# A two-layer kernel: input products issued three groups ahead in the scan layer, and the last convolution of the spectral layer on two row halves

## The chip, the cores and the metric

The kernel runs on one core of a Trainium2 chip. The metric is the device time of one execution in microseconds (us). The engines are named as in the profile: PE is TensorE (PEld its weight loads), DVE is VectorE, ACT is ScalarE, POOL is GpSimd and SP is SyncE, which here only issues DMAs.

## The reference

The input x is 4 images of 192 channels of 128 x 128, in fp32. Two residual layers follow each other, each on a group-normalised x (32 groups of 6 channels):

```python
x = x + L0(_gn(x), ...)     # spectral convolution
x = x + L1(_gn(x), ...)     # selective scan over the 16384 tokens of an image
```

The first layer (layer 1 in this text) reduces 192 channels to 48 by a 1x1 convolution. 16 of them get a 1x1 convolution, 16 a two-dimensional fractional Fourier transform, and 16 a real FFT; of both transforms magnitude and phase are convolved and transformed back. A last 1x1 convolution maps the 48 channels back to 192. The second layer (layer 2) normalises each token, projects it to 2 x 384 channels (xs and z), convolves xs along the tokens (4 taps), applies SiLU (u), computes dt, B and C from u, and runs for each of 384 channels and 16 states

```python
hnew = hcar * exp(dt_t * A) + (dt_t * u_t) * B_t
y_t  = sum over the 16 states of hnew * C_t
```

The result y + u * D is gated by SiLU(z) and projected back to 192 channels.

## The kernel before

**Layer 1** (`layer0` in the code) works image by image, a piece being 8 rows (1024 pixels of all 192 channels, 768 KB). `analysis(b)` reads the 16 pieces of an image twice: once for the statistics (`bn`), once for the first convolution (L278), whose result goes to HBM as d1. `branches(b)` computes the transforms, with several trips through HBM, and ends by writing the image dimg (L453). `synthesis(b)` reads each piece a third time, loads the 48 convolved channels and a row of ones into a tile cat (L464 to L466), multiplies it with the weights w2x (L471), adds the result to the piece (L475), takes the statistics for layer 2, and stores the piece (L477). The loop at L489 advances `branches(b)` step by step, and with it `analysis(b+1)` and `synthesis(b-1)`; here a scheduler orders the instructions of each engine. `synthesis` of the last image runs alone. Pieces come from a pool of 6 buffers.

**Layer 2** (`layer1` in the code) cuts the 4 x 16384 tokens into 128 chunks of 512. A chunk has 24 groups k, which are 3 channel tiles j by 8 pairs of states sg, so k = 8 j + sg. Here the order of every engine's queue is the order of the code (`manual_schedule`). For each state, ACT computes da = exp(dt A) (L802), DVE the scan over 512 tokens (`scans`, L872). The other input of the scan, (dt u) B, has three sources: POOL computes it for the pair as db (`inputs`, L830) in the groups 1, 4, 7, 9, 15, 17 and 23; PE transposes it back from a version that ACT scaled (`scale_pair` L846, `turned_back` L858) in the groups with sg = 3 and 6; and DVE multiplies it (`product`, L822) in the others. After a group's two scans POOL multiplies their result h with C, giving hc (L885). PE adds the hc of the 16 states into py by transposing matmuls (`sums`, L898), three groups later (LAG). `add_skip` (L912) adds u D, `evacuate` (L907) copies py to yt, `turn` (L922) turns it back, `gate` (L927) multiplies it with SiLU(z), and `finish` (L936) projects it. The tile h has 3 buffers, hc 5, db 2, and bc (the rows of B and C of a pair, spread over all partitions, L776) 8.

Into these groups the code weaves the parts of `front`, which prepares a later chunk: statistics of the tokens, projection, convolution, dt, B and C. `front` is a generator; a plain `yield` ends its part of a group, and what follows `yield MID` is issued after the group's first scan, what follows `yield LATE` at the group's end. The scaling of a chunk by its standard deviations (L660) is such a part.

What a group issues, in order, and where the distances to other groups are set:

```python
if pos >= LAG and sg != LAG:
    sums(*order[pos - LAG])
...
if pos + 2 < len(order):
    inputs(*order[pos + 2])
...
scans(pos, n, k, between)
...
if pos >= LAG and sg == LAG:
    sums(*order[pos - LAG])
    add_skip(n, j)
```

Of the kernel before, what the change touches and what calls it, by code (L numbers as in the profile page):

```python
# [19 lines left out]
C = 192  # L20
CH = 96
# [100 lines left out]
def layer0(tc, x, xmid, st2, w):  # L122

    nc = tc.nc
    B = x.shape[0]
    with ExitStack() as ctx:
        def pool(name, bufs, **kw):
            return ctx.enter_context(tc.tile_pool(name=name, bufs=bufs, **kw))

        cp = pool("l0c", 1)  # L130
        dram = pool("l0d", 2, space=DRAM)
        xp = pool("l0x", 6)
        sp = pool("l0s", 2)
        imp = pool("l0i", 2)
        zp = pool("l0z", 2)
# [13 lines left out]
        ri_cat, ri_out = const("ri_cat"), const("ri_out")  # L149


        w2x = cp.tile([3 * NC + 1, C], F32, name="w2x")
        nc.sync.dma_start(out=w2x[NC : 3 * NC, :], in_=w["w2T"][NC:, :])
# [6 lines left out]
        nc.sync.dma_start(out=w2x[0:NC, :], in_=folded[0:NC, :])  # L160
        nc.sync.dma_start(out=w2x[3 * NC :, :], in_=folded[NC:, :])
        half_pi = cp.tile([128, 1], F32, name="half_pi")
        nc.vector.memset(half_pi, math.pi / 2)

# [4 lines left out]
        dmag = []  # L169
        zrow = cp.tile([1, S], F32, name="zrow")  # L170
        nc.vector.memset(zrow, 0.0)
        orow = cp.tile([1, PIECE], F32, name="orow")
        nc.vector.memset(orow, 1.0)
# [73 lines left out]
        def analysis(b, got):  # L247


            st = sp.tile([CH, 2, NPIECE * (PIECE // 512), 6], F32, name="st")  # L250
            for p in range(NPIECE):
                bn(st, p, load(b, p))
                yield
            gst = sp.tile([CH, 2, 2], F32, name="gst")
            bn_done(st, gst)

            w1r = sp.tile([CH, 2, 128], F32, name="w1r")
            for t in range(2):  # L260
                nc.vector.tensor_scalar(w1r[:, t, :], w1T[:, t, :], gst[:, t, 1:2], None, ALU.mult)
            ps = psA.tile([128, 512], F32, name="ps")
            for t in range(2):
                nc.tensor.matmul(
                    ps[:, 0:1], w1r[:, t, :], gst[:, t, 0:1], start=t == 0, stop=t == 1
                )
            b1 = sp.tile([128, 1], F32, name="b1")
            nc.vector.tensor_scalar(b1, ps[:, 0:1], -1.0, None, ALU.mult)
            d1 = got["d1"] = dram.tile([3 * NC, S * S], F32, name="d1")
            for p in range(NPIECE):  # L270
                xt = load(b, p)
                if p % 2 == 0:
                    x1 = sp.tile([128, 2, 512], F32, name="x1")
                ps = psA.tile([128, 512], F32, name="ps")
                for t in range(2):
                    for q in range(2):
                        half = slice(64 * q, 64 * (q + 1))
                        nc.tensor.matmul(  # L278
                            ps[half], w1r[:, t, half], xt[:, t, q * 512 : (q + 1) * 512],
                            start=t == 0, stop=t == 1,  # L280
                        )
# [174 lines left out]
        def synthesis(b, got):  # L456

            d1, dimg = got["d1"], got["dimg"].rearrange("c h w -> c (h w)")
            st = sp.tile([CH, 2, NPIECE * (PIECE // 512), 6], F32, name="st2")
            for p in range(NPIECE):  # L460
                xt = load(b, p)
                cat = qp.tile([3 * NC + 1, PIECE], F32, name="cat", bufs=2)
                at = slice(p * PIECE, (p + 1) * PIECE)
                nc.sync.dma_start(out=cat[0:NC, :], in_=d1[0:NC, at])  # L464
                nc.sync.dma_start(out=cat[NC : 3 * NC, :], in_=dimg[:, at])
                nc.sync.dma_start(out=cat[3 * NC :, :], in_=orow)  # L466
                for q in range(PIECE // 512):
                    at = slice(q * 512, (q + 1) * 512)
                    pr = psB.tile([128, 2, 512], F32, name="pr")
                    for t in range(2):  # L470
                        nc.tensor.matmul(  # L471
                            pr[0:CH, t, :], w2x[:, t * CH : (t + 1) * CH], cat[:, at],
                            start=True, stop=True,
                        )
                    nc.vector.tensor_add(xt[:, :, at], xt[:, :, at], pr[0:CH])  # L475
# [12 lines left out]
        behind = iter(())  # L488
        for b in range(B):  # L489
            ahead = analysis(b + 1, got[b + 1]) if b + 1 < B else iter(())  # L490
            for i, _ in enumerate(branches(b, got[b])):
                next(ahead, None)
                next(ahead if i % 2 else behind, None)
            for rest in (behind, ahead):
                for _ in rest:
                    pass
            behind = synthesis(b, got[b])
        for _ in behind:
            pass

# [3 lines left out]
def layer1(tc, xmid, out, st2, w, n_tok=S * S):  # L504
# [2 lines left out]
    B = len(xmid)  # L507
    NCHUNK = n_tok // T
    G = 2
    LAG, FRONT, BCL = 3, 14, 5  # L510
    AHEAD = 4

    BY_POOL = ((1, 4, 7), (1, 7), (1, 7))
# [5 lines left out]
    with ExitStack() as ctx:  # L519
# [84 lines left out]
        def front(i):  # L604
# [51 lines left out]
                    rb[0:CH, q * 128 : (q + 1) * 128], sel[:, q, :], rows, start=True, stop=True  # L656
                )
            yield
            yield MID
            nc.vector.tensor_tensor(s, s, _bc(rb[0:CH], 1, 2), ALU.mult)  # L660
            yield

# [161 lines left out]
        def inputs(n, k):  # L824

            if by_pool(k):
                g = got[n]
                j, sg = divmod(k, NG)
                db = g["db", k] = scp.tile([128, G, T], F32, name="db", bufs=2)
                nc.gpsimd.tensor_tensor(db, _bc(g["dtu"][j], 1, G), g["bc", sg][:, 0], ALU.mult)  # L830
# [121 lines left out]
        def start_front(n):  # L952
            if n < total:
                fronts.append(front(n))
# [10 lines left out]
        def go_on(parts, part):  # L965

            for f in parts[part]:
                got_on = next(f, None)
                if got_on is not None:
                    parts[got_on].append(f)  # L970

        with tc.manual_schedule():
            for i in range(min(2, total)):
                load_x(i)
            for _ in front(0):
                pass
            for sg in range(NG):
                load_bc(0, sg)
            dtu_copy(0, 0)
            inputs(*order[1])  # L980
            for at in range(AHEAD):
                early(at)
            for s in range(2):
# [1 line left out]
            decay_there(2)  # L985


            start_front(1)
            for _ in range(NGR - FRONT):
                parts = {MID: [], LATE: []}  # L990
                step(fronts, parts)
                go_on(parts, MID)
                go_on(parts, LATE)
            tails = []
            for pos, (n, k) in enumerate(order):
                j, sg = divmod(k, NG)
# [9 lines left out]
                    gate(*before)  # L1006
                if sg + 1 in BY_PE:
                    turned_back(G * (pos + 1))
                if pos >= LAG and sg != LAG:
                    sums(*order[pos - LAG])  # L1010
                if k in TURNED:
                    turned(n, TURNED[k])
# [177 lines left out]
```

## Time and profile before

| | us |
|---|---|
| median of 3 executions | 11457.8 (11452.5 to 11463.0) |
| the profiled execution | 11449.6, span 11447.4 |
| layer 1, up to the last store of a piece | 1436 |
| of it, the last image's synthesis alone | 114 |
| from there to the first scan of layer 2 | 79 |
| one chunk of layer 2, of 128 | 77.5 |

The profile shows one execution. Busy time is time in which an engine has an instruction in work. The idle time before an instruction is put down to what released it, as told by semaphores; where an instruction waits for several, the last one is named.

### The profile page before, as it was taken

How to read it: one execution, taken by the hardware profiler on the slowest of the kernel's cores; microseconds unless marked ns; L12 is line 12 of the kernel's file. 1: busy time of each engine (PE TensorE's matmuls, PEld its weight loads, DVE VectorE, ACT ScalarE, POOL GpSimd, SP SyncE). 2: the span in 40 equal slices, each digit the busy share in tenths (PEclk: the TensorE clock that was granted, in tenths of full speed). 3: DMA queues.
4: the chain of work that ended last, by engine and by line, in shares of the span. 5: the costliest groups of instructions: out<-in, count | busy, mean ns of one | idle time of the engine just before them, and what ended most of it. 6: DMA issues, size and time to landing. Idle time of an engine off the chain costs nothing.

```text
span 11447.4 us, 163662 instructions
## 1 busy us (share of the span) xinstructions
PE 10543.1 (92%) x54154; PEld 7050.4 (62%) x54154; DVE 10489.8 (92%) x11072; ACT 9324.7 (81%) x17508; POOL 9806.5 (86%) x4470
## 2 busy tenths in 40 slices
PE   4777889999999999999999999999999999999998
PEld 2444456666666666666666666666666666666666
DVE  5665679999999999999999999999999999999999
ACT  2322179988988998998998998898899999889887
POOL 0000069999999999999999999999999999999999
PEclk8888789999999999999999999999999999999998
DMA  8787734334334434434433433443443443344343
GB/s 209 206 223 203 196 106 128 112 119 128 118 113 128 127 106 130 128 107 124 128 112 119 128 120 111 128 127 105 129 128 109 123 128 114 117 128 121 111 128 99
DMA packets 1339431, 1494.73 MB, mean 131 GB/s; under 512 B 903473, under 2 KB 954358, under 8 KB 1338070
## 3 DMA queue, kind: packets, MB, share of 16 engines
q1 hardware_dynamic: 1318102, 1421.34, 42.7%
q0 software_dynamic: 13312, 50.34, 1.3%
q10 hardware_dynamic: 7168, 12.59, 0.3%
q8 instruction: 429, 7.03, 0.2%
q14 instruction: 420, 3.44, 0.1%
HBM read 1325.19 MB, written 155.32 MB: 129 GB/s over the span
## 4 chain that ended last, share of the span: by engine, by line
ACT 29%; DVE 29%; PE 26%; issue 10%; POOL 3%; DMA 2%; DVEq 0%; ACTq 0%; POOLq 0%; SPq 0%
DVE h L872 21%; ACT da L802 9%; ACT dbT L846 6%; DVE op L822 6%; PE py L898 5%; PE ps L666 4%; PE ps L936 4%; PE ps L685 4%; ACT L802 3%; PE op L858 2%; POOL db L830 2%; ACT op L802 2%; PE pr L471 2%; ACT L693 1%; PE ps L655 1%
## 5 line engine op out<-in xcount | busy, mean ns | idle before, releaser
L885 POOL TENSOR_TENSOR hc<-h,bc 128x1024 f32<-128x1024 f32 x3072 | 7196.8, 2373 | 230.7 <-PE ps L922 145.6
L872 DVE TENSOR_TENSOR_SCAN h<-da,carry,op 128x512 f32<-128x512 f32 x4216 | 5202.2, 1262 | 18.7 <-ACT da L802 7.1
L898 PEld LDWEIGHTS py<-ident,hc 128*128 128x128 f32 x24576 | 3001.5, 148 | 849.3 <-issue 685.1
L898 PE MATMUL py<-ident,hc 128*128 128x128 f32 x24576 | 3404.1, 285 | 29.9 <-ACT yt L907 17.5
L802 ACT ACTIVATE da<-dt,c_A_log 128x512 f32<-128x512 f32 x4352 | 2994.6, 724 | 184.3 <-DVE h L872 163.6
L872 DVE TENSOR_TENSOR_SCAN h<-op,carry,db 128x512 f32<-128x512 f32 x1736 | 2202.3, 1269 | 119.2 <-POOL db L830 115.2
L830 POOL TENSOR_TENSOR db<-dtu,bc 128x1024 f32<-128x1024 f32 x896 | 2136.3, 2384 | 5.6 <-DMA bc<-dbc 5.6
L822 DVE TENSOR_TENSOR op<-dp,bc 128x512 f32<-128x512 f32 x2816 | 1889.9, 671 | 32.2 <-ACT dp L785 32.2
L802 ACT ACTIVATE op<-dt,c_A_log 128x512 f32<-128x512 f32 x1792 | 1223.2, 683 | 679.7 <-DVE h L872 674.4
L846 ACT ACTIVATE dbT<-ps,bT 128x128 f32<-128x128 f32 x6144 | 1660.3, 381 | 0.0
L666 PE MATMUL ps<-s,c_wiT 96*128 96x512 f32 x3072 | 1520.9, 619 | 2.6 <-DVE s L660 2.6
L685 PE MATMUL ps<-xs,dcw 128*128 128x512 f32 x3072 | 1424.3, 592 | 1.5 <-ACT u L693 1.3
L858 PE MATMUL op<-ident,dbT 128*128 128x128 f32 x6144 | 1076.2, 295 | 109.9 <-DVE h L872 75.5
L858 PEld LDWEIGHTS op<-ident,dbT 128*128 128x128 f32 x6144 | 779.8, 151 | 405.5 <-ACT dbT L846 208.7
L666 PEld LDWEIGHTS ps<-s,c_wiT 96*128 96x128 f32 x3072 | 558.1, 199 | 467.2 <-issue 462.9
L802 ACT ACT_TABLE_LOAD x636 | 816.0, 1283 | 11.2
L685 PEld LDWEIGHTS ps<-xs,dcw 128*128 128x128 f32 x3072 | 532.9, 190 | 434.1 <-issue 432.1
L936 PE MATMUL ps<-yg,c_woT 128*96 128x512 f32 x1536 | 710.5, 598 | 71.1 <-DVE xm L942 70.9
L477 POOL DMA_DIRECT2D xmid<-xt x64 | 42.8, 668 | 788.1 <-DVE xt L475 781.3
L745 PE MATMUL ps<-xd,c_dtT 12*128 12x512 f32 x768 | 514.1, 761 | 164.5 <-DVE s L622 99.7
L936 PEld LDWEIGHTS ps<-yg,c_woT 128*96 128x96 f32 x1536 | 239.8, 163 | 437.8 <-issue 320.7
L754 POOL TENSOR_TENSOR dtu<-dt,u 128x512 f32<-128x512 f32 x384 | 479.4, 1282 | 29.6 <-ACT dt L750 29.6
(172 smaller groups left out, 10372.6 us busy)
## 6 DMA issues: line engine op xcount, KB each, us to landing
bc<-dbc SPq DMA_DIRECT2D x1024, 1024.0 KB, 5.9
xt<-in_x SPq DMA_DIRECT2D x192, 768.0 KB, 9.0
xmid<-xt POOLq DMA_DIRECT2D x64, 768.0 KB, 7.0
xm<-xmid SPq DMA_DIRECT2D x128, 384.0 KB, 3.5
carry<-h SPq DMA_DIRECT2D x3072, 1.0 KB, 1.9
out<-xm SPq DMA_DIRECT2D x128, 384.0 KB, 3.3
d<-x ACTq DMA_DIRECT2D x64, 192.0 KB, 7.1
df<-u SPq DMA_DIRECT2D x16, 512.0 KB, 5.2
```

Source lines behind the costliest of these rows:

```text
L666: nc.tensor.matmul(pp, wiT[:, t, m * 128 : (m + 1) * 128], s[:, t, :], start=t == 0, stop=t == 1)
L685: nc.tensor.matmul(pc, dcw[:, j, k, :], xs[:, j, k : k + T], start=k == 0, stop=k == 3)
L745: nc.tensor.matmul(d[j], dtT[rows, :], xd[rows, :], start=True, stop=True)
L802: nc.scalar.activation(da, got[n]["dt"][j], AF.Exp, scale=A[:, j, st : st + 1])
L822: nc.vector.tensor_tensor(dbs[s], g["dp"], g["bc", k % NG][:, 0, q, :], ALU.mult)
L830: nc.gpsimd.tensor_tensor(db, _bc(g["dtu"][j], 1, G), g["bc", sg][:, 0], ALU.mult)
L846: nc.scalar.activation(t[:, blk, :], g["tu", j][:, blk, :], AF.Identity, scale=g["bT"][:, blk, st : st + 1],)
L858: nc.tensor.transpose(db[:, blk * 128 : (blk + 1) * 128], t[:, blk, :], ident)
L872: nc.vector.tensor_tensor_scan(h[:, q, :], das.pop(s), dbs.pop(s) if db is None else db[:, q, :], 0.0 if ch == 0 else g["before"][:, j, st ...
L885: nc.gpsimd.tensor_tensor(hc, h, g["bc", sg][:, 1], ALU.mult)
L898: nc.tensor.matmul(py[:, blk, :], hc[:, q, blk * 128 : (blk + 1) * 128], ident, start=first, stop=sg == NG - 1 and q == G - 1 and blk == T ...
L936: nc.tensor.matmul(po[0:CH], woT[:, j, t * CH : (t + 1) * CH], g["yg", j], start=j == 0, stop=j == NJ - 1,)
```

## The change

In layer 2:

- `inputs`, the product db on POOL, is issued three groups ahead of its scan instead of two.
- `sums` comes at the head of every group; before, it came at the end in the groups with sg = 3. `add_skip` stays at the end of those.
- The scaling L660 moves from after the first scan of its group to the group's end.
- The rows bc are loaded one group earlier (BCL 6 for 5).
- Before the first chunk's groups, the first ten steps of the second chunk's `front` are issued among the last part of the first chunk's, not after it.

In layer 1:

- cat becomes a tile of 128 partitions by 512: the first 512 pixels of a piece lie in the partitions from 0, the other 512 in those from 64, each with a row of ones that is set once. w2x is there twice in the same way. The matmuls of the last convolution read one half each and write a bank each, and the addition takes one half of the channels and all 1024 pixels.
- In `analysis`, the last 4 pieces of the first reading stay in their buffers for the second. The pool has 7 buffers.
- In the last image's stage `synthesis` of the image before advances at every step, and after step 18 four pieces of the last image are loaded.

```diff
-        xp = pool("l0x", 6)
+        xp = pool("l0x", 7)
...
+        cats = [cp.tile([128, 512], F32, name=f"cat{i}") for i in range(2)]
+        for cat in cats:
+            nc.vector.memset(cat, 1.0)
...
             for p in range(NPIECE):
-                bn(st, p, load(b, p))
+                xt = load(b, p)
+                if p >= NPIECE - KEEP:
+                    kept[p] = xt
+                bn(st, p, xt)
                 yield
...
-            for p in range(NPIECE):
-                xt = load(b, p)
+            for p in (*range(NPIECE - KEEP, NPIECE), *range(NPIECE - KEEP)):
+                xt = kept.pop(p, None) or load(b, p)
...
-                xt = load(b, p)
-                cat = qp.tile([3 * NC + 1, PIECE], F32, name="cat", bufs=2)
-                at = slice(p * PIECE, (p + 1) * PIECE)
-                nc.sync.dma_start(out=cat[0:NC, :], in_=d1[0:NC, at])
-                nc.sync.dma_start(out=cat[NC : 3 * NC, :], in_=dimg[:, at])
-                nc.sync.dma_start(out=cat[3 * NC :, :], in_=orow)
-                for q in range(PIECE // 512):
-                    at = slice(q * 512, (q + 1) * 512)
+                xt = early[p] if p < len(early) else load(b, p)
+                cat = cats[p % 2]
+                for q in range(2):
+                    at = slice(p * PIECE + q * 512, p * PIECE + (q + 1) * 512)
+                    nc.sync.dma_start(out=cat[64 * q : 64 * q + NC, :], in_=d1[0:NC, at])
+                    nc.sync.dma_start(out=cat[64 * q + NC : 64 * q + 3 * NC, :], in_=dimg[:, at])
+                for t in range(2):
                     pr = psB.tile([128, 2, 512], F32, name="pr")
-                    for t in range(2):
+                    for q in range(2):
+                        rows = slice(64 * q, 64 * q + 3 * NC + 1)
                         nc.tensor.matmul(
-                            pr[0:CH, t, :], w2x[:, t * CH : (t + 1) * CH], cat[:, at],
+                            pr[0:CH, q, :], w2x[rows, t * CH : (t + 1) * CH], cat[rows, :],
                             start=True, stop=True,
                         )
...
-                next(ahead if i % 2 else behind, None)
+                next(ahead if i % 2 and b < B - 1 else behind, None)
+                if b == B - 1 and i == LOADS:
+                    early = [load(b, p) for p in range(KEEP)]
...
-    LAG, FRONT, BCL = 3, 14, 5
+    LAG, FRONT, BCL = 3, 14, 6
...
-            yield MID
+            yield LATE
             nc.vector.tensor_tensor(s, s, _bc(rb[0:CH], 1, 2), ALU.mult)
...
-            for _ in front(0):
-                pass
-            for sg in range(NG):
-                load_bc(0, sg)
+            first = [front(0)]
+            for i in range(2 * NGR - FRONT):
+                if i == NGR - 6:
+                    start_front(1)
+                once(first)
+                if NGR - 6 <= i < 2 * NGR - FRONT - 6:
+                    once(fronts)
+                if i == NGR + 1:
+                    for sg in range(NG):
+                        load_bc(0, sg)
...
-                if pos >= LAG and sg != LAG:
+                if pos >= LAG:
                     sums(*order[pos - LAG])
...
-                if pos + 2 < len(order):
-                    inputs(*order[pos + 2])
+                if pos + 3 < len(order):
+                    inputs(*order[pos + 3])
...
-                if pos >= LAG and sg == LAG:
-                    sums(*order[pos - LAG])
+                if sg == LAG:
                     add_skip(n, j)
```

More of the change, by code (lines that the diff above doesn't have):

```diff
@@ L125, in layer0 @@
     B = x.shape[0]
+    KEEP = 4
+    LOADS = 18
     with ExitStack() as ctx:
@@ L149, in layer0 @@
         ri_cat, ri_out = const("ri_cat"), const("ri_out")
-        w2x = cp.tile([3 * NC + 1, C], F32, name="w2x")
-        nc.sync.dma_start(out=w2x[NC : 3 * NC, :], in_=w["w2T"][NC:, :])
+        w2x = cp.tile([128, C], F32, name="w2x")
+        for q in range(2):
+            nc.sync.dma_start(out=w2x[64 * q + NC : 64 * q + 3 * NC, :], in_=w["w2T"][NC:, :])
         w20, c0 = cp.tile([NC, C], F32, name="w20"), const("c0")
@@ L159, in layer0 @@
         nc.vector.tensor_copy(folded, ps[0 : NC + 1, 0:C])
-        nc.sync.dma_start(out=w2x[0:NC, :], in_=folded[0:NC, :])
-        nc.sync.dma_start(out=w2x[3 * NC :, :], in_=folded[NC:, :])
+        for q in range(2):
+            nc.sync.dma_start(out=w2x[64 * q : 64 * q + NC, :], in_=folded[0:NC, :])
+            nc.sync.dma_start(
+                out=w2x[64 * q + 3 * NC : 64 * q + 3 * NC + 1, :], in_=folded[NC:, :]
+            )
         half_pi = cp.tile([128, 1], F32, name="half_pi")
@@ L171, in layer0 @@
         nc.vector.memset(zrow, 0.0)
-        orow = cp.tile([1, PIECE], F32, name="orow")
-        nc.vector.memset(orow, 1.0)
+        cats = [cp.tile([128, 512], F32, name=f"cat{i}") for i in range(2)]
+        for cat in cats:
+            nc.vector.memset(cat, 1.0)
         for i in range(min(2, B)):
@@ L250, in analysis @@
             st = sp.tile([CH, 2, NPIECE * (PIECE // 512), 6], F32, name="st")
+            kept = {}
             for p in range(NPIECE):
-                bn(st, p, load(b, p))
+                xt = load(b, p)
+                if p >= NPIECE - KEEP:
+                    kept[p] = xt
+                bn(st, p, xt)
                 yield
@@ L454, in branches, with synthesis @@
             got.update(dimg=dimg)
-        def synthesis(b, got):
+        def synthesis(b, got, early):
             d1, dimg = got["d1"], got["dimg"].rearrange("c h w -> c (h w)")
@@ L460, in synthesis @@
             for p in range(NPIECE):
-                xt = load(b, p)
-                cat = qp.tile([3 * NC + 1, PIECE], F32, name="cat", bufs=2)
-                at = slice(p * PIECE, (p + 1) * PIECE)
-                nc.sync.dma_start(out=cat[0:NC, :], in_=d1[0:NC, at])
-                nc.sync.dma_start(out=cat[NC : 3 * NC, :], in_=dimg[:, at])
-                nc.sync.dma_start(out=cat[3 * NC :, :], in_=orow)
-                for q in range(PIECE // 512):
-                    at = slice(q * 512, (q + 1) * 512)
+                xt = early[p] if p < len(early) else load(b, p)
+                cat = cats[p % 2]
+                for q in range(2):
+                    at = slice(p * PIECE + q * 512, p * PIECE + (q + 1) * 512)
+                    nc.sync.dma_start(out=cat[64 * q : 64 * q + NC, :], in_=d1[0:NC, at])
+                    nc.sync.dma_start(out=cat[64 * q + NC : 64 * q + 3 * NC, :], in_=dimg[:, at])
+                for t in range(2):
                     pr = psB.tile([128, 2, 512], F32, name="pr")
-                    for t in range(2):
+                    for q in range(2):
+                        rows = slice(64 * q, 64 * q + 3 * NC + 1)
                         nc.tensor.matmul(
-                            pr[0:CH, t, :], w2x[:, t * CH : (t + 1) * CH], cat[:, at],
+                            pr[0:CH, q, :], w2x[rows, t * CH : (t + 1) * CH], cat[rows, :],
                             start=True, stop=True,
                         )
-                    nc.vector.tensor_add(xt[:, :, at], xt[:, :, at], pr[0:CH])
+                    nc.vector.tensor_add(
+                        xt[:, t, :], xt[:, t, :], pr[0:CH].rearrange("p q f -> p (q f)")
+                    )
                 bn(st, p, xt)
@@ L490, in layer0 @@
             ahead = analysis(b + 1, got[b + 1]) if b + 1 < B else iter(())
+            early = []
             for i, _ in enumerate(branches(b, got[b])):
                 next(ahead, None)
-                next(ahead if i % 2 else behind, None)
+                next(ahead if i % 2 and b < B - 1 else behind, None)
+                if b == B - 1 and i == LOADS:
+                    early = [load(b, p) for p in range(KEEP)]
             for rest in (behind, ahead):
@@ L496, in layer0 @@
                     pass
-            behind = synthesis(b, got[b])
+            behind = synthesis(b, got[b], early)
         for _ in behind:
@@ L970, in go_on, with once @@
                     parts[got_on].append(f)
+        def once(works):
+            parts = {MID: [], LATE: []}
+            step(works, parts)
+            go_on(parts, MID)
+            go_on(parts, LATE)
         with tc.manual_schedule():
@@ L974, in layer1 @@
                 load_x(i)
-            for _ in front(0):
-                pass
-            for sg in range(NG):
-                load_bc(0, sg)
+            first = [front(0)]
[8 more added lines that the diff above has]
+                        load_bc(0, sg)
+            assert not first, first
             dtu_copy(0, 0)
-            inputs(*order[1])
+            for at in order[1:3]:
+                inputs(*at)
             for at in range(AHEAD):
@@ L985, in layer1 @@
             decay_there(2)
[L988 to L993, printed above, removed]
             tails = []
```

## Prediction

> **What bounds the kernel now.** I read the page first, then the windows by stage, then the timelines of layer 2 on POOL and DVE, its waits, and the two places where layer 1 hands over to layer 2.
>
> ```profile
> span 11447.4 us, 163662 instructions
> PE 10543.1 (92%) x54154; PEld 7050.4 (62%) x54154; DVE 10489.8 (92%) x11072; ACT 9324.7 (81%) x17508; POOL 9806.5 (86%) x4470
> ...
> L885 POOL TENSOR_TENSOR hc<-h,bc 128x1024 f32<-128x1024 f32 x3072 | 7196.8, 2373 | 230.7 <-PE ps L922 145.6
> ...
> L830 POOL TENSOR_TENSOR db<-dtu,bc 128x1024 f32<-128x1024 f32 x896 | 2136.3, 2384 | 5.6 <-DMA bc<-dbc 5.6
> ```
>
> The averages mix two layers. Layer 1 takes the first 1437 us; layer 2 then runs 128 equal chunks, 77.5 us from one to the next. Windows of busy time (columns: length, PE, PEld, DVE, ACT, POOL busy, granted clock, DMA share, GB/s), first the end of layer 1, then ten chunks:
>
> ```profile
> 1320.00:1434.00 114.00, 109.51 (x128) 35.67 (x128) 79.42 (x98) 0.00 (x0) 10.11 (x16) 0.50 0.73 214
> 3000.00:3775.00 775.00, 739.35 (x3968) 505.80 (x3967) 752.71 (x781) 700.55 (x1331) 758.25 (x341) 0.95 0.40 121
> ```
>
> A chunk has 75.8 us on POOL, 75.3 on DVE, 73.9 on PE. So no engine has more than 3.6 us to spare, and the waits decide. POOL over two thirds of a chunk (start, duration):
>
> ```profile
> 5028.23 2.41 POOL L830 TENSOR_TENSOR db<-dtu,bc 128x1024 f32<-128x1024 f32 x1
> 5030.56 9.37 POOL L885 TENSOR_TENSOR hc<-h,bc 128x1024 f32<-128x1024 f32 x4
> 5040.35 2.37 POOL L885 TENSOR_TENSOR hc<-h,bc 128x1024 f32<-128x1024 f32 x1 [0.43 <-DVE h L872]
> 5043.92 2.36 POOL L885 TENSOR_TENSOR hc<-h,bc 128x1024 f32<-128x1024 f32 x1 [1.19 <-PE ps L922]
> 5046.23 2.40 POOL L830 TENSOR_TENSOR db<-dtu,bc 128x1024 f32<-128x1024 f32 x1
> 5048.59 4.70 POOL L885 TENSOR_TENSOR hc<-h,bc 128x1024 f32<-128x1024 f32 x2
> 5053.25 2.37 POOL L830 TENSOR_TENSOR db<-dtu,bc 128x1024 f32<-128x1024 f32 x1
> 5055.59 6.97 POOL L885 TENSOR_TENSOR hc<-h,bc 128x1024 f32<-128x1024 f32 x3
> ```
>
> I number a chunk's 24 groups k = 0 to 23. These are db(9), hc(7) to (10), hc(11), hc(12), db(15), hc(13) and (14), db(17), hc(15) to (17). POOL stops twice, 0.43 + 1.19 = 1.6 us. The releaser PE L922 of the second had nothing for it; scan(12) on DVE ended at 5043.75, 0.17 before, so both stops are waits for DVE. DVE in turn waits (columns: us in total, times, longest; 103 chunks):
>
> ```profile
> DVE s L660 <- PE ps L655: 114.2, 103, 1.2
> DVE h L872 <- POOL db L830: 96.4, 277, 0.7
> ```
>
> That is 1.11 us a chunk at L660 (k = 22) and 0.94 for db at k = 4, 7 and 9. The loop that sets 77.5 us: db(9) ends at 5030.64, scan(9) starts at 5030.68, DVE runs without a gap to hc(12), and POOL without a gap on to the next db(9).
>
> **What the skill says.** (1) "TensorE: Matmul & The Clock Gate", Part 3: matmuls in different row or column tiles run at the same time. The column tiles of L278 agree: 512 records of 672 ns lie in 141.5 us of busy time, so two at once. Row tiles of 64 no run here shows; I take the same factor of 2, with bounds 1 and 2. (2) The same page, Part 1: the clock is either half or full, and stays half without enough activity. In the tail of layer 1 the clock is 0.50 although PE is 96% busy, so it is no mere question of gaps; I keep half speed. (3) "DMA: Bandwidth & Descriptors", Issuing engines are not separate DMA queues: all share 16 engines. The tail's 214 GB/s at share 0.73, and 261 at 0.96 in the first 126 us, fit one common limit.
>
> **The change, part by part.**
>
> *db one group earlier (56 us gained).* In seven groups (1, 4, 7, 9, 15, 17, 23) db(k) is now issued ahead of hc(k-3) instead of behind it. It moves no DMA. But h has three buffers: scan(k) overwrites the tile that hc(k-3) reads. Before, POOL ran hc(6), db(9), then scan(9) started; now db(9), hc(6), and scan(9) waits for hc(6), which ends when db(9) did. So the 0.94 us of DVE's wait for db stay, under another name. What gains is POOL: db(15) comes ahead of hc(12) and fills its 1.19 us. Replay, with pitches of 2.33: hc(11) still starts at 5040.35; db(15) to 5045.0, hc(12) 5047.3, hc(13) 5049.7, db(17) 5052.0, hc(14) 5054.3, hc(15) 5056.7; hc(16) waits 0.1 for scan(16), which ends 5056.65; hc(17) would start at 5059.1 but scan(17) ends at 5059.60, so it starts at 5059.75. Before it started at 5055.59 + 6.97 - 2.37 = 5060.19. The rest of POOL's chunk runs on without a stop, so the next chunk comes 0.44 us sooner: 77.06. Times 127: 56 us. All 1.6 us would be 208; the lower end is 0 if hc(17)'s slack is less than one chunk shows. hc(k-3) is read 2.33 us later in those groups by PE's sums (L898); the nearest, sums(6), starts 3.4 us after hc(6) ended, so it has 1.1 left.
>
> *L660 to the group's end (0).* Its 1.11 us vanish behind scan(22), but DVE then reaches the waits at k = 4, 7, 9 earlier and waits there for POOL. On PE, L666 after it starts 2 us later than L660 ends, so nothing behind is late.
>
> *Sums at the head of groups 3, 11, 19 (0, bounds 0 and 3 us a chunk).* They pass L685 (half), L666, and L836 with L760 on PE, and wait for the copy of py (L907). In one chunk PE reaches the three places 10.2, 35.4 and 62.0 us in; the copies end at 10.2, 35.1 and 62.1. They just fit.
>
> *bc one group earlier (0).* Eight 1 MB loads a chunk, 5.9 us each. Each waits on SP for an hc two groups back and holds up the carry DMAs; SP waited only 55 us in 103 chunks there, and those hc still end before the group's scans.
>
> *Layer 2's start (7).* Before:
>
> ```profile
> 1499.65 0.67 ACT L802 ACTIVATE op<-dt,c_A_log 128x512 f32<-128x512 f32 x1
> 1500.26 1.50 ACT L612 ACTIVATE s<-xm,nmr,st 96x512 f32<-96x512 f32 x2
> ...
> 1514.16 1.22 DVE L660 TENSOR_TENSOR s<-s,ps 96x1024 f32<-96x1024 f32 x1 [2.83 <-PE ps L655]
> 1515.30 2.32 DVE L872 TENSOR_TENSOR_SCAN h<-da,op 128x512 f32<-128x512 f32 x2
> ```
>
> The first scan waits 15.1 us for ten steps of the second chunk's front part. These now lie among the first chunk's. PE is nearly full there: L619 3.7, L635 3.6, L647 0.4, L655 2.0 and L666 1.9 us come to 11.6, less some 3 of its gaps. 15 - 8 = 7; bounds 0 and 15.
>
> *Last convolution on two row halves (38 + 22).* Each piece keeps four matmuls, but two and two run together. In the tail PE needs 8 x 0.853 = 6.83 us a piece and is the bound. At half that (3.4), DVE is next: 79.4/16 = 5.0 us. DMA: with four pieces loaded ahead and seven buffers, 9 loads and 16 stores of 0.786 MB and 3.1 MB of cat, 22.8 MB at 261 GB/s, take 87 us. With 5 us to fill: 92 instead of 114, gain 22 (bounds 10 and 34). The 64 loads of a constant row go; 64 more SP issues of cat at 0.4 us come, spread over 1300 us, hidden by SP's waits. In the three stages before, L471 holds 7.6%, 7.3% and 9.6% of the chain over 304, 304 and 320 us: 23 + 22 + 31 = 76, half of it 38 (bounds 0 and 60). That synthesis of image 2 now ends sooner in the last stage, I count in these.
>
> *Pieces kept (4).* 16 of 192 loads go, 12.6 MB or 48 us at 261 GB/s. But four of seven buffers are held at the turn, so only three, not six, load ahead; in the first analysis 9 loads remain instead of 10: about 4. In later stages DMA is 0.68 to 0.85 busy; 0, bounds -10 and +12 for each.
>
> **Sum.** 56 + 7 + 38 + 22 + 4 = 127 us. The profiled execution took 11449.6 with a span of 11447.4, 8 below the median of 11457.8; the same saving from that median gives 11331.
>
> **Rivals.** *Layer 2 gains nothing:* another scan's wait takes hc(17)'s place. For it: 0.44 us is small beside 77.5; against it: the replay has no other stop. Then 71 us remain, 11387; with only half of layer 1, 11420. *POOL never stops:* DVE's path from 9 to 17 would have to shrink by 1.2 us; nothing in the diff does that. 208 for 56: 11179. *Slower:* the sums at the heads of groups 3, 11 and 19 hold PE until py is copied. PE has 3.6 us idle in a chunk; if the three waits take over 3 us together (ACT copying 1 us later each time), scans that need PE's op (k = 3, 6) fall behind, and PE sets the pace. At 5 us the chunk grows by about 1.5: +192 - 71, or 11579. It decides from 3 us on. *The row halves don't overlap:* the 38 and most of the 22 go; 11385.
>
> **How the numbers follow.** Forecast 0.55, layer 2 without gain 0.2, no overlap 0.08, POOL never stopping 0.09, slower 0.08. The forecast's own range is 11275 to 11390. The range 11215 to 11425 leaves out the slow case, the full POOL case and a little more. About 0.2%, 23 us, is what a measurement of this kernel can tell from no change: faster 0.87, same 0.05, slower 0.08.
>
> **What would show it.** After: DVE's L872 waits for POOL hc, not db, at k = 4, 7, 9, still about 1 to 2 us a chunk; POOL stops before hc(11) and, by half a us, before hc(17), no longer before hc(12); L660 waits for nothing; the first scan comes 7 us sooner after layer 1; L471's records pair up. A chunk of 77.5 or more, or PE L898 waiting for ACT L907 by more than 1 us a chunk, would prove me wrong.

## The result, and the profile after

The changed kernel takes 11509.8 us (median of 5, 11497.7 to 11520.9), the kernel before 11457.8 on the same chip. The ratio is 1.0043, with a 95% interval of 1.0029 to 1.0058: slower by 0.4%, where 11331 and "faster" were forecast.

The lines of the kernel have moved by 18 in layer 2: the scan L872 is now L890, hc L885 is L903, db L830 is L848, the sums L898 are L916, the copy of py L907 is L925, L836 and L760 are L854 and L778, the copy of bT L763 is L781, L642, L645, L655 and L660 are L660, L663, L673 and L678. So L660 is now the square root (L642 before), and the scaling, L660 before, is L678. In layer 1 the last convolution L471 is L484. From the page, the lines that answer to those of before:

```profile
span 11507.8 us, 163611 instructions
PE 10451.9 (91%) x54154; PEld 7096.1 (62%) x54154; DVE 10485.1 (91%) x11073; ACT 9298.0 (81%) x17507; POOL 9823.4 (85%) x4470
...
L903 POOL TENSOR_TENSOR hc<-h,bc 128x1024 f32<-128x1024 f32 x3072 | 7198.9, 2365 | 321.4 <-DVE h L890 205.5
...
L848 POOL TENSOR_TENSOR db<-dtu,bc 128x1024 f32<-128x1024 f32 x896 | 2142.2, 2391 | 4.7 <-DMA bc<-dbc 4.7
```

The work is the same: the two POOL groups take the same time to within 0.3%. What grew is the idle time ahead of hc, from 230.7 to 321.4 us. The span is 60.4 us longer, and two numbers from the trace split it. The first scan starts at 1453.2 us instead of 1515.3: layer 1 and the start of layer 2 gained 62. The mean distance between chunks is 78.45 us instead of 77.48: 127 times 0.96 is 122 lost. 122 - 62 = 60.

So layer 2 is what went wrong. Its waits between 2000 and 10000 us, 102 chunks (us in total, times, longest):

```profile
PE py L916 <- ACT yt L925: 188.8, 175, 1.3
ACT bT L781 <- PE ps L778: 224.6, 102, 2.5
DVE rs L663 <- ACT rs L660: 126.3, 87, 2.1
DVE yg L945 <- PE ps L940: 87.1, 102, 1.4
DVE h L890 <- PE op L876: 78.6, 77, 1.4
```

All five were next to nothing before (ACT waited 5.8 us in all for L760, PE 12.3 for the copy at L907, DVE 2.2 at the gate, 0.8 for PE's op and nothing for the root); DVE's wait at the scaling, 1.11 us a chunk before, is gone as forecast, and so is its wait for db. They fall in two places of the chunk. In group 3 PE waits 0.8 us a chunk for the copy of py, and then DVE waits 0.85 at the gate L945 for PE's L940. The rest is one story, which begins in group k = 19. PE (start, duration, what ended the idle time before):

```profile
5044.88 1.94 PE L916 MATMUL py<-ident,hc 128*128 128x128 f32 x8 [1.26 <-ACT yt L925]
5046.61 1.06 PE L854 MATMUL ps<-ident,dtu 128*128 128x128 f32 x4
5047.47 0.90 PE L778 MATMUL ps<-ident,xd 128*128 128x128 f32 x4
...
5052.42 0.60 PE L876 MATMUL op<-ident,dbT 128*128 128x128 f32 x4
...
5053.73 0.60 PE L876 MATMUL op<-ident,dbT 128*128 128x128 f32 x4
```

ACT:

```profile
5044.17 0.56 ACT L925 COPY yt<-py 128x512 f32<-128x512 f32 x1
5044.64 1.34 ACT L820 ACTIVATE da<-dt,c_A_log 128x512 f32<-128x512 f32 x2
5048.40 0.21 ACT L781 COPY bT<-ps 128x64 f32<-128x64 f32 x1 [2.43 <-PE ps L778]
5048.64 1.28 ACT L660 ACT_TABLE_LOAD   x1
5049.93 0.26 ACT L660 ACTIVATE rs<-ps,eps 128x4 f32<-128x4 f32 x1
...
5053.57 1.34 ACT L820 ACTIVATE da<-dt,c_A_log 128x512 f32<-128x512 f32 x2
```

DVE:

```profile
5050.23 0.18 DVE L663 RECIPROCAL rs<-rs 128x4 f32<-128x4 f32 x1 [1.47 <-ACT rs L660]
5050.34 2.45 DVE L890 TENSOR_TENSOR_SCAN h<-da,carry,op 128x512 f32<-128x512 f32 x2
5052.70 0.66 DVE L945 TENSOR_TENSOR yg<-ps,zs 128x512 f32<-128x512 f32 x1
5054.39 2.45 DVE L890 TENSOR_TENSOR_SCAN h<-da,carry,op 128x512 f32<-128x512 f32 x2 [1.02 <-PE op L876]
```

PE waits 1.26 us for the copy of py, then issues eight sums, and only then the transposes L854 and L778. After its copy of py ACT has two exponentials to compute, and next in the order of the code is the copy of what L778 writes. So for 2.43 us ACT stands there, and behind it stand the square root L660 and the exponentials of later groups. DVE's reciprocal waits for that root 1.47 us and holds up DVE's own scans.

The exponentials themselves come late too. The first scan of group 22, at 5054.39, is put down to PE's L876, but that is not what it waited for: the four transposes for this scan, at 5052.42, had ended at 5053.02, and those that end at 5054.33 are for the group's second scan. What ended last was the scan's own exponential da, the first of the two at 5053.57, which was done at 5054.30. Sorted in this way by what each scan reads, the first scan of group 22 waits 1.0 us a chunk for ACT. The stop at L678, where one would look first because the change touched it, is gone.

### The profile page after: what moved, and what is told of

It is laid out like the page before. It is cut to its first block, busy times and chain, and to the rows that moved or that the text cites. A ratio compares the mean times of both kernels' runs of the same rounds, so it can differ in the third digit from the quotient of the medians.

```text
span 11507.8 us, 163611 instructions
## 1 busy us (share of the span) xinstructions
PE 10451.9 (91%) x54154; PEld 7096.1 (62%) x54154; DVE 10485.1 (91%) x11073; ACT 9298.0 (81%) x17507; POOL 9823.4 (85%) x4470
## 4 chain that ended last, share of the span: by engine, by line
ACT 41%; DVE 32%; PE 14%; issue 9%; DMA 2%; POOL 1%; DVEq 0%; SPq 0%; ACTq 0%; POOLq 0%
DVE h L890 23%; ACT da L820 11%; ACT dbT L864 7%; DVE op L840 6%; ACT L820 5%; ACT op L820 4%; PE py L916 4%; ACT L711 3%; PE ps L684 2%; ACT zs L715 2%; ACT u L711 2%; ACT L660 1%; PE ps L703 1%; ACT L715 1%; ACT dp L803 1%
## 5 line engine op out<-in xcount | busy, mean ns | idle before, releaser
L903 POOL TENSOR_TENSOR hc<-h,bc 128x1024 f32<-128x1024 f32 x3072 | 7198.9, 2365 | 321.4 <-DVE h L890 205.5
L890 DVE TENSOR_TENSOR_SCAN h<-da,carry,op 128x512 f32<-128x512 f32 x4216 | 5198.8, 1263 | 126.5 <-PE op L876 92.3
L916 PE MATMUL py<-ident,hc 128*128 128x128 f32 x24576 | 3451.7, 288 | 251.8 <-ACT yt L925 234.2
L916 PEld LDWEIGHTS py<-ident,hc 128*128 128x128 f32 x24576 | 3019.9, 150 | 1045.4 <-issue 886.7
L890 DVE TENSOR_TENSOR_SCAN h<-op,carry,db 128x512 f32<-128x512 f32 x1736 | 2197.7, 1266 | 16.4 <-POOL hc L903 2.4
L848 POOL TENSOR_TENSOR db<-dtu,bc 128x1024 f32<-128x1024 f32 x896 | 2142.2, 2391 | 4.7 <-DMA bc<-dbc 4.7
L684 PE MATMUL ps<-s,c_wiT 96*128 96x512 f32 x3072 | 1475.7, 603 | 5.2 <-ACT xs L697 3.6
L703 PE MATMUL ps<-xs,dcw 128*128 128x512 f32 x3072 | 1447.7, 593 | 0.0
L876 PE MATMUL op<-ident,dbT 128*128 128x128 f32 x6144 | 1068.1, 294 | 26.5 <-DVE h L890 13.5
L876 PEld LDWEIGHTS op<-ident,dbT 128*128 128x128 f32 x6144 | 782.5, 150 | 287.0 <-ACT dbT L864 147.1
L820 ACT ACT_TABLE_LOAD x635 | 814.7, 1283 | 11.2
L684 PEld LDWEIGHTS ps<-s,c_wiT 96*128 96x128 f32 x3072 | 527.6, 192 | 387.8 <-issue 379.9
L763 PE MATMUL ps<-xd,c_dtT 12*128 12x512 f32 x768 | 440.8, 656 | 149.1 <-ACT dbT L864 76.7
L930 PEld LDWEIGHTS py<-ddp,u 128*128 128x128 f32 x3072 | 403.6, 196 | 121.8 <-issue 121.8
```

Of the source, the lines that this page charges most:

```text
L684: nc.tensor.matmul(pp, wiT[:, t, m * 128 : (m + 1) * 128], s[:, t, :], start=t == 0, stop=t == 1)
L703: nc.tensor.matmul(pc, dcw[:, j, k, :], xs[:, j, k : k + T], start=k == 0, stop=k == 3)
L820: nc.scalar.activation(da, got[n]["dt"][j], AF.Exp, scale=A[:, j, st : st + 1])
L876: nc.tensor.transpose(db[:, blk * 128 : (blk + 1) * 128], t[:, blk, :], ident)
L890: nc.vector.tensor_tensor_scan(h[:, q, :], das.pop(s), dbs.pop(s) if db is None else db[:, q, :], 0.0 if ch == 0 else g["before"][:, j, st ...
L903: nc.gpsimd.tensor_tensor(hc, h, g["bc", sg][:, 1], ALU.mult)
```

## The experiments

Times are medians in us, each against the kernel before on the same chip in the same session. "Chunk" is the mean distance between chunks in the profiled execution, "first scan" when layer 2's first scan started.

| kernel | median | before | ratio (95%) | chunk | first scan |
|---|---|---|---|---|---|
| before | 11457.8 | | | 77.48 | 1515 |
| after | 11509.8 | 11457.8 | 1.0043 (1.0029 to 1.0058) | 78.45 | 1453 |
| e1_sums_end | 11319.6 | 11453.4 | 0.9881 (0.9864 to 0.9897) | 77.01 | 1445 |
| e2_sums_end19 | 11314.6 | 11453.4 | 0.9879 (0.9864 to 0.9893) | 77.01 | 1441 |
| e3_only_sums | 11582.0 | 11453.4 | 1.0110 (1.0095 to 1.0125) | 78.50 | 1526 |
| e4_layer1_only | 11389.0 | 11453.4 | 0.9943 (0.9928 to 0.9957) | 77.48 | 1456 |
| e5_only_db | 11401.6 | 11463.7 | 0.9945 (0.9931 to 0.9960) | 77.04 | 1518 |
| e8_bT_later | 11347.9 | 11463.7 | 0.9899 (0.9884 to 0.9913) | 77.18 | 1449 |
| e9_h4 | 11246.4 | 11463.7 | 0.9809 (0.9793 to 0.9825) | 76.42 | 1452 |
| e10_before_h4 | 11461.4 | 11463.7 | 1.0000 (0.9991 to 1.0008) | 77.55 | 1520 |
| e6_only_scale | 11452.0 | 11458.9 | 0.9995 (0.9986 to 1.0004) | 77.44 | 1522 |
| e11_no_kept | 11393.8 | 11458.9 | 0.9944 (0.9929 to 0.9958) | 77.48 | 1458 |
| e12_no_halves | 11457.4 | 11458.9 | 1.0001 (0.9992 to 1.0010) | 77.49 | 1534 |
| e13_h4_sums_end | 11162.0 | 11458.9 | 0.9741 (0.9727 to 0.9756) | 75.75 | 1441 |

The first scan of the one profiled execution moves by up to 13 us between kernels that have the same code up to there (1515 to 1526 with that of before, 1441 to 1453 with that of the changed kernel), so layer 1 is judged by the medians.

### Which part of the change costs the time

**e1_sums_end**, the changed kernel with the sums of groups 3, 11 and 19 back at their end:

```diff
-                if pos >= LAG:
+                if pos >= LAG and sg != LAG:
                     sums(*order[pos - LAG])
...
-                if sg == LAG:
+                if pos >= LAG and sg == LAG:
+                    sums(*order[pos - LAG])
                     add_skip(n, j)
```

> The changed kernel with one edit undone: in the groups with sg = 3 the sums come at the group's end again. Theory (the sums at the head of group 19, and less those of group 3, hold PE until ACT has copied py, and with PE the transposes L778, ACT's copy of bT behind them and DVE's L663): the chunk falls from 78.58 to the 77.06 us of the prediction's replay, so 11510 - 127 x 1.52 = 11317, within 11300 to 11340. Rival (the later hc of the seven groups starve PE, or h's buffers DVE): the chunk stays above 78 and the time above 11440.

11319.6: all the harm, and the whole difference to the forecast, is in this one edit. Its waits (104 chunks):

```profile
DVE h L890 <- POOL hc L903: 128.3, 268, 0.9
PE py L916 <- ACT yt L925: 10.9, 33, 0.4
ACT bT L781 <- PE ps L778: 5.8, 26, 0.2
```

ACT no longer stands at L781, and DVE waits for hc, not db. On average POOL stops 0.42 us before hc(11), 0.12 before hc(16) and 0.57 before hc(17).

**e2_sums_end19**, the same, but only the sums of group 19 at the end; those of 3 and 11 stay at the head:

```diff
-                if pos >= LAG:
+                if pos >= LAG and k != NGR - 5:
                     sums(*order[pos - LAG])
...
                 if sg == LAG:
                     add_skip(n, j)
+                    if k == NGR - 5:
+                        sums(*order[pos - LAG])
```

> The changed kernel with the sums at the end in group 19 alone, and at the head in groups 3 and 11. Theory that group 19 alone does the harm (1.26 us of PE there, 2.2 us of ACT behind it): as the kernel with all three at the end, 11317 to 11340. If group 3 (0.95 us of PE, and DVE's L945 0.85 us late) counts too: between, 11370 to 11450. Rival that it is the db: above 11440.

11314.6, as good as e1, though PE still waits 0.65 us a chunk for the copy of py, 0.54 of it in group 3. With the sums of group 19 at the end, those at the head of groups 3 and 11 cost nothing.

**e3_only_sums**, the kernel before with nothing but the sums moved to the heads.

```diff
-                if pos >= LAG and sg != LAG:
+                if pos >= LAG:
                     sums(*order[pos - LAG])
...
-                if pos >= LAG and sg == LAG:
-                    sums(*order[pos - LAG])
+                if sg == LAG:
                     add_skip(n, j)
```

> The kernel before, with nothing but the sums moved to the head of the groups with sg = 3. Theory: PE waits for the copy of py as in the changed kernel, the chunk grows from 77.5 to 78.4 to 79.0 us, 11458 + 127 x 0.9 to 1.5 = 11570 to 11650. Rival (db or the scaling to blame): 11458 plus or minus 10.

11582.0: this edit alone costs 129 us, 1.02 us a chunk. Its waits (102 chunks; line numbers of before):

```profile
POOL hc L885 <- DVE h L872: 150.0, 206, 2.0
ACT bT L763 <- PE ps L760: 112.5, 102, 2.6
DVE h L872 <- ACT da L802: 103.3, 128, 1.0
PE py L898 <- ACT yt L907: 9.2, 11, 1.3
```

The time is in the range that was expected, but not by the way that was expected: PE hardly waits for the copy of py here, 0.1 us a chunk. The eight sums by themselves, about 1 us ahead of L836 and L760, are enough. ACT stands 1.1 us at the copy of bT in every chunk, and DVE's scan of group 22 waits 1.0 us for the exponential behind it, as in the changed kernel. One chunk, ACT and PE:

```profile
5043.27 0.56 ACT L907 COPY yt<-py 128x512 f32<-128x512 f32 x1
...
5046.14 0.21 ACT L763 COPY bT<-ps 128x64 f32<-128x64 f32 x1 [1.07 <-PE ps L760]
```

```profile
5044.16 1.07 PE L898 MATMUL py<-ident,hc 128*128 128x128 f32 x8
...
5045.51 0.60 PE L760 MATMUL ps<-ident,xd 128*128 128x128 f32 x4
```

In the changed kernel ACT's stop is twice as long, 2.2 us a chunk, and the clock has a part in it. In the chunk shown above the granted clock was 0.54 from 5044.88 to 5048.37, while PE did the eight sums (1.94 us) and the eight transposes; in e3 it was 1.00 from 5044.16 to 5046.11. Why the clock is lower there, after PE's wait, no run takes apart.

**e8_bT_later** puts this to the test from the other side. It is the changed kernel, all sums at the heads, with ACT's copy of bT issued one group later and nothing else moved:

```diff
+            yield
+            z1 = in_proj(NJ + 1)
             yield LATE
             g["bT"] = tp.tile([128, T // 128, NS], F32, name="bT")
             nc.scalar.copy(g["bT"], bt.rearrange("p (k c) -> p k c", c=128)[:, :, 96 : 96 + NS])
             yield
-            z1 = in_proj(NJ + 1)
-            yield
             yield
```

(A `yield` ends a group's part, so z1 stays in its group and the copy comes to the end of that group.)

> The changed kernel, sums at the head of all groups, with one edit: ACT's copy of bT (L781), which waits for PE's L778, is issued one group later, at the end of group 20. PE's wait for the copy of py stays. Theory A (what costs is ACT standing in its queue before L781, since the sums pass L778): chunk 77.1 to 77.5, 11315 to 11370. Theory B (what costs is PE's own wait for py): chunk 78 or more, above 11440.

11347.9. PE still waits for the copy of py, 0.8 us a chunk and more than in e2, and yet the chunk falls from 78.45 to 77.18 (104 chunks):

```profile
PE py L916 <- ACT yt L925: 85.3, 98, 1.3
DVE yg L945 <- PE ps L940: 113.8, 150, 2.5
DVE h L890 <- PE op L876: 103.7, 100, 1.9
PE ps L665 <- ACT bT L783: 102.0, 86, 1.7
```

So letting ACT go on at that copy gives back 1.27 of the 1.44 us by which the changed kernel is worse than e1. PE's wait for py did not stay what it was, though: it fell from 1.85 to 0.82 us a chunk. That the harm doesn't need this wait is shown by e3, not here. The remaining 0.17 us were not taken apart. The later copy has a wait of its own, the last line: PE's L665 stands 1.0 us a chunk until ACT has read bT, since both use the three buffers of ps.

### The other parts, one at a time

**e4_layer1_only**: layer 1 of the changed kernel with layer 2 of the kernel before.

> The first layer of the changed kernel with the second layer of the kernel before. In the changed kernel's profile the last piece of layer 1 is stored 55 us sooner; nothing in layer 2 hangs on it, so 11458 - 55 = 11403, within 11395 to 11410.

11389.0, 64 us less than before, and below the range expected. That range came from two single profiled executions; the medians differ by more.

**e5_only_db**: the kernel before with db three groups ahead and bc one group earlier.

```diff
-    LAG, FRONT, BCL = 3, 14, 5
+    LAG, FRONT, BCL = 3, 14, 6
...
-            inputs(*order[1])
+            for at in order[1:3]:
+                inputs(*at)
...
-                if pos + 2 < len(order):
-                    inputs(*order[pos + 2])
+                if pos + 3 < len(order):
+                    inputs(*order[pos + 3])
```

> The kernel before with the products db alone issued three groups ahead (and bc a group earlier, which they need). Theory: the loop over hc(17), scan(9) to scan(17) holds no L660, so the chunk is 77.06 us with this edit alone, 11453 - 56 = 11397, within 11385 to 11410. Rival (the scaling had its part): 11420 to 11450.

11401.6, 62 us less, 0.45 us a chunk. DVE waits for hc instead of db, 0.49 us a chunk; at L660 it still waits its 1.1 in this kernel.

**e6_only_scale**: the kernel before with L660 at its group's end.

```diff
-            yield MID
+            yield LATE
             nc.vector.tensor_tensor(s, s, _bc(rb[0:CH], 1, 2), ALU.mult)
```

> The kernel before with only the scaling L660 moved to its group's end. Theory: its 1.1 us of DVE's wait go, DVE waits so much longer for POOL's db at k = 4, 7 and 9, and the time stays: 11460 plus or minus 12. Rival (DVE is the bound): 11460 - 127 x 1 = 11330.

No change: 0.9995. DVE's 1.1 us at L660 go and come back at once as a wait for db:

```profile
DVE h L872 <- POOL db L830: 200.2, 384, 1.2
```

200.2 us against 96.4 before, 104 more, where 114 had gone. In this kernel taking a wait from DVE gains nothing; POOL sets the pace.

**e11_no_kept**: e4 without the kept and early pieces and with 6 piece buffers.

```diff
-    KEEP = 4
+    KEEP = 0
...
-        xp = pool("l0x", 7)
+        xp = pool("l0x", 6)
```

> Layer 2 of the kernel before; layer 1 of the changed kernel with no pieces kept, none loaded ahead and 6 buffers, that is, the row halves (and the faster advance of the synthesis in the last stage) alone. Theory: the row halves give most of the 64 us of layer 1: 11400 to 11420. Rival (kept and early pieces give most): 11435 to 11455.

**e12_no_halves**: e4 with the old convolution (cat of 49 x 1024, w2x once, one addition per 512 pixels) and 6 buffers, so only the kept and early pieces and the advance in the last stage remain. Against e4:

```diff
-        xp = pool("l0x", 7)
+        xp = pool("l0x", 6)
...
-                cat = cats[p % 2]
+                cat = qp.tile([3 * NC + 1, PIECE], F32, name="cat", bufs=2)
...
-                            pr[0:CH, q, :], w2x[rows, t * CH : (t + 1) * CH], cat[rows, :],
+                            pr[0:CH, t, :], w2x[:, t * CH : (t + 1) * CH], cat[:, at],
```

> Layer 2 of the kernel before; layer 1 of the changed kernel with the last convolution as before, over 49 rows and 1024 columns, and 6 buffers; the pieces are kept and loaded ahead. Theory: PE stays the bound of the last synthesis at 6.8 us a piece and the four kept buffers save little: 11435 to 11465. Rival: 11400 to 11420.

11393.8 and 11457.4: the row halves (with the advance in the last stage, which both kernels have) are all of layer 1's 64 us, the kept pieces nothing. e11 came 6 us below its expected range, e12 within it.

### What bounds layer 2 next

**e9_h4**: e2 with four buffers for h instead of three; hc gets four instead of five.

```diff
-            h = scp.tile([128, G, T], F32, name="h", bufs=3)
+            h = scp.tile([128, G, T], F32, name="h", bufs=4)
...
-            hc = scp.tile([128, G, T], F32, name="hc", bufs=5)
+            hc = scp.tile([128, G, T], F32, name="hc", bufs=4)
```

> The kernel with sums at the end in group 19 alone, h with 4 buffers instead of 3 and hc with 4 instead of 5[...]. Theory: scan(9) waits for h's buffer, not for db, so with a fourth it starts up to 2.3 us sooner, DVE is ahead of hc(11), (16) and (17), and POOL stops no more: chunk 75.9 to 76.2, 11315 - 127 x 1.0 = 11188, within 11165 to 11215. Rival (another wait takes its place within the 1.1 us: ACT's da, PE's op, or hc's missing buffer): 11230 to 11315.

11246.4: 217 us less than before, where e2 had 139 less, with DVE's wait for hc gone, but not down to the 11165 to 11215 of POOL without a stop: the time lies in the rival's range. Another wait has its place, DVE's gate behind PE:

```profile
DVE yg L945 <- PE ps L940: 101.7, 105, 1.5
PE py L916 <- ACT yt L925: 64.6, 83, 1.1
```

**e10_before_h4**: the same two lines in the kernel before.

> The kernel before with h in 4 buffers and hc in 4. Theory: before, DVE waits for db, which POOL works on two groups ahead, not for h, so nothing changes: 11453 plus or minus 12. Rival (h's buffers bound the kernel before too): 11350 or less. A loss above 11465 would mean that the missing buffer of hc costs.

11461.4, no change. Where db itself is late, a fourth h is of no use. Neither line was tried without the other.

**e13_h4_sums_end**: e1 with the two lines, so that PE doesn't wait for the copy of py in group 3 either.

> As the kernel with four h buffers before it, but with the sums at the end in group 3 too (and 11), as before the change. That kernel's chunk was 76.48, and DVE waited 0.97 us a chunk at L945, which waits for PE's L940, late behind the wait for py in group 3. Theory: that wait goes, DVE is no longer the bound, POOL's last stop of 0.5 us at hc(17) goes with it: chunk 75.9 to 76.1, 11246 - 127 x 0.45 = 11189, within 11170 to 11215. Rival (POOL and DVE limit each other anyway): 11235 to 11255.

11162.0, 2.6% below the kernel before and the best of all; a little better than expected. The sums at the heads of groups 3 and 11, free in e2, cost 0.67 us a chunk once POOL could use it. Windows of ten chunks (length, PE, PEld, DVE, ACT, POOL busy, clock, DMA share, GB/s), the changed kernel first:

```profile
3000.00:3770.00 770.00, 727.76 (x3919) 505.15 (x3918) 738.48 (x766) 684.42 (x1304) 745.82 (x335) 0.95 0.42 121
```

and e13:

```profile
3000.00:3770.00 770.00, 744.39 (x4010) 509.80 (x4009) 763.43 (x793) 710.12 (x1352) 769.68 (x347) 0.95 0.41 121
```

POOL is busy 769.68 of 770 us, and a chunk takes 75.75 us, which is the work that POOL has in it (75.8 in the kernel before). Now POOL is the bound; any further step in layer 2 would have to take work from it.

## Why the prediction was wrong

**The step that failed** is "Sums at the head of groups 3, 11, 19 (0, bounds 0 and 3 us a chunk)". It named L836 and L760 as instructions that the sums are moved past, and then asked only whether PE itself would find py copied: "They just fit." Two things were wrong in it.

First, who waits for L760 was not asked. ACT's copy of bT comes after it. In these traces ACT comes to that copy 1.24 us after the end of its copy of py (in all kernels but e8). In one chunk of the kernel before, PE, then ACT:

```profile
5065.84 0.60 PE L760 MATMUL ps<-ident,xd 128*128 128x128 f32 x4
```

```profile
5065.02 0.57 ACT L907 COPY yt<-py 128x512 f32<-128x512 f32 x1
...
5066.72 0.20 ACT L763 COPY bT<-ps 128x64 f32<-128x64 f32 x1
```

L760 ended at 5066.44, ahead of ACT. Over the 103 chunks of the kernel before, it ended 0.57 us ahead on average, and in 26 chunks ACT already had to wait a little. With the sums at the head, L836 and L760 can't start until py is copied and eight sums are done. In e3 L760 ends 2.3 us after the copy of py on average, against the 1.24 us that ACT has. ACT waits 1.1 us, though PE hardly waits at all, and this alone costs 1.02 us a chunk.

Second, the fit was between 62.0 and 62.1 us in a chunk in which db had not yet been moved. For the sums alone it held (e3, 0.1 us of waiting). In the changed kernel PE waits 1.26 us at that place in the chunk shown and 1.0 on average. The step used a timeline of before to vouch for a margin of a tenth of a us.

Both signs of being wrong that the prediction named came: a chunk above 77.5 us, 78.45, and PE waiting for the copy by more than 1 us a chunk, 1.85.

**The slower rival** had the place right and the mechanism and the price wrong. It put the point of decision at over 3 us of PE waiting for the copy, because PE has 3.6 us idle. In the changed kernel PE waits 1.85 us a chunk for it, in e3 0.1, and both are slower in layer 2. PE's idle time was no measure: the idle time that mattered was ACT's slack at one instruction. Its chance of 0.08 was too low for an edit with a margin that small.

**What held.** db three groups ahead: 56 us forecast, chunk 77.06; e1 has 77.01, e5 77.04 and 62 us. The stops of the replay (0.43 before hc(11), 0.1 before hc(16), about half a us before hc(17), none before hc(12)) are those of e1. That the h buffer would take db's place in DVE's waits is seen in e1, e5 and e9. L660 at the group's end: 0 forecast, 0 measured (e6). Start of layer 2: 7 forecast; from the start of the last store to the first scan it is 77.0 us instead of 84.0. With the sums left where they were, the forecast of 11331 stands beside 11319.6. So every other term of layer 2 held.

**Layer 1** came to the 64 us forecast, but in other portions, so that the sum fits is luck. Up to the write of the last dimg the kernels with the new layer 1 gained 21 to 27 us (after, e4, e1), and of these 16 to 23 in the three stages with a synthesis, where the row halves were put at 38; the tail gained 34 (from that write to the last store, 128.7 to 95.1 us), where 22 were given. The kept pieces gained 0 for 4: in e11, without them, the first dimg comes 12 us later than in e4, but the last one at the same time (1277.2 and 1277.9 us).

Why the stages gave less than 38 is not shown. One candidate is that the faster advance in the last stage costs time by itself: in e12, which has it without the row halves, that stage took 291 us, against 270 to 274 in the kernels with the old layer 1 and 263 to 266 with the new. But the profiled execution of e12 was 14 us above its median.

The tail's gain has two parts. From the write of dimg to the first matmul of the last synthesis it is 10.6 us instead of 17.7, and 11.2 in e12: this is not the row halves, and the prediction had no term for it. From there to the last store it is 84.5 us instead of 111.1, and 111.1 in e12: here the row halves gave 27 us instead of 22. DMA was put at a limit of 261 GB/s; the tail after shows that this was not the limit:

```profile
1298.00:1377.00 79.00, 62.17 (x116) 20.07 (x112) 70.53 (x90) 0.00 (x0) 9.73 (x16) 0.50 0.89 272
```

DMA moves 272 GB/s at a share of 0.89. The 22.8 MB of the forecast would take 84 us at that rate instead of 87, so this is only a part of the 5. Nor did the forecast's two figures give one limit: taken to a share of 1, 261 GB/s at 0.96 is 272, and 214 at 0.73 is 293 (estimates). DVE is busy 70.5 of 79 us, 4.4 us a piece, and a piece takes 4.9: the tail now runs near DVE's pace.

## What to carry to other kernels

When an instruction is moved ahead of others in an in-order queue, list for each one that it passes who waits for it and how much that engine has to spare at that instruction, not in the whole chunk. The waits table does not give this: the 0.06 us a chunk that ACT waited for L760 said nothing of how soon it would wait more. And where the table names a releaser, look in the timeline whether the waiting instruction reads what that one writes: the wait put down to PE's L876 was one for ACT. Put a margin of a tenth of a microsecond from one profiled chunk down as a coin toss, above all where other edits shift the same chunk. And free one buffer or move one group only with the next wait in view: the same fourth h was worth nothing, 78 us and 163 us in three orders of the same queues (e10, e9 against e2, e13 against e1, each measured from its own kernel before).

## What was not expected of the hardware

Two row tiles gave a factor of 1.80. The prediction had taken 2 from the column tiles of L278. The Trainium skill, "TensorE: Matmul & The Clock Gate", Part 3, which says that tiles run at the same time, gives 3.07 for four row tiles and nothing for two. Here the eight matmul records of a piece (two for each of its four matmuls) in the tail of the changed kernel, in fp32 with 49 of 64 rows used, take

```profile
1340.86 3.80 PE L484 MATMUL pr<-cat,w2x 49*96 49x512 f32 x8 [1.40 <-DVE xt L488]
```

3.80 us instead of 6.83. The clock was 0.50 in this tail too, with or without the halves, so the clock has no part in the gain. It agrees with the page's Part 1, by which the clock is either half or full, in so far as the clock records of all these runs hold 0.5 and 1.0 alone.
